# Which matmuls stand at the beginning of a step: reordering the work around a state-space scan

## The chip, the cores and the metric

One core of one Trainium2 chip runs the whole program. The metric is the device time of one execution in microseconds, the median of several runs. Beside it stands one execution taken by the hardware profiler; its page and its trace are what the text quotes.

## The reference, cut to what matters

Four layers with a residual sum around each, on x of 8 x 384 x 32 x 32 in fp32. Each layer first normalizes in 32 groups (`_gn`).

```python
def _mamba(xseq, ...):                      # layer 0; layer 2 adds a layer norm before and an MLP after
    xz = xseq @ in_proj_w.T
    xin, z = jnp.split(xz, 2, axis=-1)      # 768 channels each
    u = silu(conv3(xin))                    # causal, three taps
    dt, Bm, Cm = split(u @ x_proj_w.T)
    dt = softplus(dt @ dt_proj_w.T + dt_proj_b)
    A = -jnp.exp(A_log)                     # 768 x 16
    def step(h, inp):                       # over the 1024 positions
        h = exp(dt_t[..., None] * A) * h + (dt_t * u_t)[..., None] * B_t[:, None, :]
        return h, einsum('bdn,bn->bd', h, C_t)
    y = (ys + u * D) * silu(z)
    return y @ out_proj_w.T

x = x + layer0(_gn(x))                      # _mamba
x = x + layer1(_gn(x))                      # 1x1, 8x8 rfft filter, 3x3 depthwise, gelu gate, 1x1
x = x + layer2(_gn(x))                      # layer norm, _mamba, MLP with gelu
x = x + layer3(_gn(x))                      # 3x3 depthwise
```

## The kernel before, in words

**Chunks and steps.** A layer of the `_mamba` kind is cut into 16 chunks: 8 images of 2 halves of 512 positions. A chunk has 24 steps (NQ), so the two such layers have 768 steps. A step holds 32 channels with their 16 states each, as four tiles of 128 rows by 512 positions. The first half of an image leaves its last states in `carry` for the second.

**One step** has these parts, written in this order by the loop at the end of the function, which is the order on every engine (nothing is rescheduled):

- `times(t+1)`: GpSimd multiplies the loaded dt·u of the next step by B (two products of 2.36 us).
- `scan(t)`: VectorE runs four `tensor_tensor_scan` on the decays dA0 to dA3 (PSUM tiles), multiplies the first two results by C; GpSimd multiplies the other two (L660).
- `jobs.begin`, then `jobs.step(t, 2.0)`: up to about 2 us of TensorE work of other jobs.
- `gather(t-1)`: TensorE sums the states of the step before into y (four matmuls of 32 columns); every fourth step it adds u·D, and VectorE multiplies by the gate z (L676).
- `begin(t+3)`: SyncE loads g, a 1 MB broadcast of the step three ahead, from `dud`. If that step's dt isn't computed yet, `jobs.until` writes whatever job pieces are due first, until it is.
- `jobs.step(t)`: more pieces of other jobs.
- `decay(t+1)`: TensorE spreads dt into dA0 to dA3, ScalarE takes the exponentials in place.

There is one set of dA tiles: the decays of the next step wait for the scans and products of this one.

**Other jobs** are Python generators; a piece runs to the next `yield`. `measure` and `group_stats` take group statistics; `front` is the normalization, in-projection (ps_in, emptied by ScalarE into u, then two tap operations of VectorE), Silu, x-projection (ps_x, dbc), spreading of B and C (ps_bc) and the softplus of dt (ps_dt, three ScalarE operations, then VectorE's dt; GpSimd's du; the write to `dud`); `gates` is z; `finish` is the out-projection and the MLP (ps_up emptied by ScalarE, ps_dn by VectorE); `layer1` and `layer3` are the convolutional layers (ps_t, ps_dw, ps_o). Layer 1 and layer 3 of an image run beside later chunks.

`Jobs` keeps them in the order of their due step (`last`). It meters the TensorE and VectorE work that is written (`work`), and a step has room for so much of either (ROOM). `step` starts a job's next piece where the room is at least what that piece took the last time. The yields are: WAIT (cannot go on), NEXT (go on in the next step), EARLY (go on at the beginning of the next step: Silu and Gelu, with the loading of their ScalarE tables), and None.

**Banks.** Other work has three PSUM banks (`psg`, NBANK = 3). `pipe` passes units through their stages with a bank each, at most `deep` at a time; `live["ps"]` counts the banks that are taken, and `ps_done` counts one free when the instruction that empties it has been written. Only the semaphores, at run time, make a matmul wait for the emptying itself.

Of the kernel before, what the change touches and what calls it, by code (L numbers as in the profile page):

```python
# [48 lines left out]

SHARE = {"l0_": ((2, 2, 2, 2), (2, 2, 2, 2)), "l2_": ((2, 2, 2, 2), (2, 2, 2, 2))}  # L50
# [15 lines left out]
EARLY = "early"  # L66

ROOM = {"l0_": (5.2, 3.0), "turn": (6.4, 3.0), "l2_": (6.4, 3.0)}
# [21 lines left out]
class Jobs:  # L90
# [3 lines left out]

    def __init__(self, work):
        self.work, self.jobs, self.needs = work, [], {}
        self.room = [0.0, 0.0]

    def add(self, kind, gen, first, last):
        self.jobs.append({"kind": kind, "gen": gen, "first": first, "last": last, "had": [], "got": None})  # L100
# [5 lines left out]
    def piece(self, job):  # L106

        before = list(self.work)
        got = next(job["gen"], self)
        if got is WAIT:  # L110
            return False
        took = tuple(x - y for x, y in zip(self.work, before))
        job["had"].append(took)
        self.room = [x - y for x, y in zip(self.room, took)]
        job["got"] = got
        if got is self:
            self.needs[job["kind"]] = job["had"]
            self.jobs.remove(job)
        return True
# [4 lines left out]
    def begin(self, room):  # L124
        self.room = [max(min(x, y / 8), -y) + y for x, y in zip(self.room, room)]
        early = [job for job in self.in_order() if job["got"] is EARLY]
        for job in self.jobs:
            if job["got"] is NEXT:
                job["got"] = None
        if early:  # L130
            self.piece(early[0])

    def step(self, t, most=None):

        most = most and self.work[0] + most
        went = True
        while went and not (most and self.work[0] >= most):
            went = False
            for job in self.in_order():
                need = self.need(job)  # L140
                if job["got"] is None and job["first"] <= t and all(
                    y == 0 or x >= y - 0.1 for x, y in zip(self.room, need)
                ):
                    went = self.piece(job)
                    if went:
                        break

    def until(self, done):

        while not done():  # L150
            if not any(self.piece(job) for job in self.in_order()):
                raise RuntimeError("no job goes on")


@with_exitstack
def tile_conv_preact_d4(ctx: ExitStack, tc: tile.TileContext, a: dict, out: bass.AP):
# [10 lines left out]
    live = {"ps": 0, "dt": 0, "x": 0, "spm": False}  # L167
# [21 lines left out]
    def pipe(units, deep=2):  # L189


        flying = []
        units = deque(units)
        while units or flying:
            went = bool(flying)
            for f in list(flying):
                if f["stages"]:
                    f["stages"].popleft()(f["ps"])
                settle(f)
                if not f["stages"]:  # L200
                    flying.remove(f)
            if units and live["ps"] < NBANK and len(flying) < deep:
                went = True
# [3 lines left out]
                stages[0](ps)  # L207
                f = {"stages": deque(stages[1:]), "ps": ps, "bank": True}
                settle(f)
                if f["stages"]:  # L210
                    flying.append(f)
            if units or flying:
                yield None if went else WAIT

    def settle(f):
        if f["bank"] and (not f["stages"] or f["stages"][0] is None):
            f["bank"] = False
            ps_done()
            if f["stages"]:
                f["stages"].popleft()  # L220
# [59 lines left out]
    def group_stats(block, all_read=lambda: None, between=None):  # L280
# [3 lines left out]
        for h in range(2):  # L284
            for k in range(KC):
                v, then = block(h, k)
                vector.bn_stats(st[:, k, h, :], v)
                then()
# [75 lines left out]
    def depthwise(pool, rows, todo):  # L364
# [13 lines left out]
        for q, (n, t) in enumerate(taps):  # L378
            if t == 0:
                ps = yield from ps_tile("ps_dw")  # L380
            _, window, take = todo[n]
            ready.append(diagonal(q + 3))
            mm(
# [6 lines left out]
            if t % 3 == 2:  # L390
                yield
# [7 lines left out]
    def measure(s):  # L399
# [12 lines left out]
        live["spm"] = True  # L412
# [7 lines left out]
        def all_read():  # L420
            live["spm"] = False
# [3 lines left out]
    def project(s, d, at):  # L425


        def run(ps):
            for k in range(KC):
                mm(  # L430
                    ps,
                    s["w"]["in"][:, k, at + d * P : at + (d + 1) * P],
                    s["xn"][:, k, :],
                    start=k == 0,
                    stop=k == KC - 1,
                )

        return run

    def gates(s, h):  # L440
# [7 lines left out]
        def evict(d):  # L448
# [3 lines left out]
            ("ps_z", [both(project(s, h * NH + d, DI), evict(d))]) for d in range(NH)  # L452
        )
        yield EARLY
# [5 lines left out]
    def layer_norm(xn):  # L460
        ps = yield from ps_tile("ps_ln")
        for k in range(KC):
            mm(ps, ln_mean, xn[:, k, :], start=k == 0, stop=k == KC - 1)
# [4 lines left out]
        while live["spm"]:  # L468
            yield WAIT
        ps = yield from ps_tile("ps_lv")  # L470
        for k in range(KC):
            sq = wk.tile([P, T], F32, tag="spm", name="sq", bufs=2)
            act(sq, xn[:, k, :], AF.Square)
            mm(ps, ln_mean, sq, start=k == 0, stop=k == KC - 1)
        rsqrt(ps, ps, eps_ln)
        yield
# [8 lines left out]
        yield NEXT  # L485

    def front(s):

        c, n = s["c"], s["n"]
        while n > 0 and ("gates", 1) not in chunks[n - 1]:  # L490
# [28 lines left out]
        def taps(d):  # L519
# [9 lines left out]
        yield from pipe(  # L529
            ("ps_in", [both(project(s, d, 0), tap(d), taps(d))]) for d in range(ND)  # L530
        )
# [19 lines left out]
        for d in range(ND):  # L551
            mm(ps[:RX, :], w["x"][:, d, :], u[d], start=d == 0, stop=d == ND - 1)
        dbc = wk.tile([RX, T], F32, tag="dbc", name="dbc")
        act(dbc, ps[:RX, :], AF.Identity, bias=one_row)
        ps_done()
        yield NEXT
# [9 lines left out]
        def step_dt(d):  # L566
# [10 lines left out]
            def plus(ps):  # L577
                v = s["dt"][d] = wk.tile([P, T], F32, tag="dt", name="dt", bufs=NDT)
                vector.scalar_tensor_tensor(v, ps, 0.0, got["m"], ALU.max, ALU.add)

# [11 lines left out]
            return [both(log, plus), None, both(times_u, spill)]  # L592
# [3 lines left out]
        flying = []  # L596
        for d in range(ND):
            while live["dt"] >= NDT or live["spm"]:
                yield WAIT
            live["dt"] += 1  # L600

            flying.append(pipe([("ps_dt", step_dt(d))]))
            flying = [f for f in flying if next(f, f) is not f]
            yield NEXT
        while flying:
            flying = [f for f in flying if next(f, f) is not f]
            yield NEXT
# [29 lines left out]
    def scan(s, i):  # L637

        g = s["g", i]
        own = SHARE[s["pre"]][s["c"]][i % NSUB]  # L640
        for j in range(4):
            q = 4 * i + j
            nc.vector.tensor_tensor_scan(  # L643
                dAs[j] if j < own else g[:, j, :],
# [6 lines left out]
            if j < own:  # L651
                if s["c"] < NCH - 1:
                    nc.vector.tensor_copy(carry[:, q : q + 1], dAs[j][:, T - 1 : T])
                nc.vector.tensor_mul(g[:, j, :], dAs[j], s["bc"][:, 1, :])  # L654
        if s["c"] < NCH - 1:
            nc.vector.tensor_copy(  # L656
                carry[:, 4 * i + own : 4 * i + 4].unsqueeze(2), g[:, own:4, T - 1 : T]
            )
        g = g[:, own:4, :]
        nc.gpsimd.tensor_mul(  # L660
            g, g, s["bc"][:, 1, :].unsqueeze(1).to_broadcast([P, 4 - own, T])
        )

    def gather(s, i):
# [8 lines left out]
        if sub == NSUB - 1:  # L673
            u = s["u"][k // NH][:, k % NH, :]
            mm(y, s["w"]["D"][:, k, :], u, start=False)
            nc.vector.tensor_mul(u, y, s["z", k // NH][:, k % NH, :])  # L676
# [4 lines left out]
    def out_proj(s):  # L681
# [14 lines left out]
        def part(m, h):  # L696
            def run(ps):
                for d in range(h * NH, (h + 1) * NH):
# [474 lines left out]
```

## Time and profile before

| what | value |
|---|---|
| median of 3 runs | 7934.5 us (7925.13 to 7950.72) |
| the profiled execution | 7942.61 us, its span 7940.8 us |
| mean granted TensorE clock | 0.919 of full rate |
| TensorE busy | 7334.3 us, 92% |
| VectorE busy | 5717.7 us, 72% |
| GpSimd busy | 5639.5 us, 71% |
| ScalarE busy | 4052.0 us, 51% |
| DMA queues | 57.2% of 16 engines' span, 1117.98 MB on SyncE's |
| g loads (1 MB each) | 768, 7.1 us from issue to landing |

The span runs from the first instruction to the last; the time of the execution is 1.8 us longer. A matmul's end is modelled, and one that waits behind another is counted busy, so the share of TensorE is no measure of how full it is. An fp32 matmul has two records in the trace. Lines of the program are those of the kernel before; L177 is the helper `mm`, L85 the metered VectorE call, L241 the helper `act`, so the tiles' names tell operations apart.

### The profile page before, as it was taken

The numbers are of one execution on the slowest core, as the hardware profiler recorded it, in microseconds if no ns is written. First come the engines' busy times: TensorE is split into PE (matmuls) and PEld (weight loads), VectorE is DVE, ScalarE is ACT, GpSimd is POOL, SyncE is SP. The second block draws the span as 40 slices with busy tenths as digits, with TensorE's granted clock in tenths as the row PEclk, the third lists the DMA queues.
The fourth block names the chain that finished last, engine by engine and source line by source line (L and its number), as shares of the span: only waits on it lengthen the run. The fifth ranks groups of instructions, "written<-read, shape, count | busy, mean of one in ns | idle before, by whom it ended". The sixth has DMA issues, their size and how long they took to land. (4 is left out here: it accounts for less than half of the span.)

```text
span 7940.8 us, 76871 instructions
## 1 busy us (share of the span) xinstructions
PE 7334.3 (92%) x25954; PEld 3037.2 (38%) x25954; DVE 5717.7 (72%) x7254; ACT 4052.0 (51%) x6980; POOL 5639.5 (71%) x2710
## 2 busy tenths in 40 slices
PE   7989999999998999989999989999899989999898
PEld 2223333333333333333334444444444444344445
DVE  5988788878787878778737647767767676676770
ACT  4445545555555555554544545555555555555553
POOL 5888888877787878777737746767767667676770
PEclk8888888989898999989889989999999999999999
DMA  5665655555564656556526645666656666565662
GB/s 138 148 148 137 144 135 136 134 133 137 133 149 118 146 129 143 122 141 151 122 69 173 159 121 144 154 158 165 157 134 163 166 149 159 138 171 140 168 157 65
DMA packets 289704, 1122.90 MB, mean 141 GB/s; under 512 B 37402, under 2 KB 91754, under 8 KB 191004
## 3 DMA queue, kind: packets, MB, share of 16 engines
q1 hardware_dynamic: 289308, 1117.98, 57.2%
q8 instruction: 205, 3.36, 0.2%
q14 instruction: 191, 1.56, 0.1%
HBM read 1042.34 MB, written 75.50 MB: 141 GB/s over the span
## 5 line engine op out<-in xcount | busy, mean ns | idle before, releaser
L623 POOL TENSOR_TENSOR g<-g,bc 128x1024 f32<-128x1024 f32 x1536 | 3586.5, 2357 | 181.3 <-DMA g<-dud 164.4
L660 POOL TENSOR_TENSOR g<-g,bc 128x1024 f32<-128x1024 f32 x768 | 1805.8, 2351 | 1609.5 <-DVE carry L656 871.8
L241 ACT ACTIVATE dA<-dA,w_A 128x512 f32<-128x512 f32 x3072 | 1858.3, 661 | 1480.3 <-PE dA L177 1467.3
L177 PE MATMUL dA<-dt,selr 32*128 32x512 f32 x6144 | 1521.9, 676 | 67.8 <-DVE g L654 59.2
L643 DVE TENSOR_TENSOR_SCAN dA<-dA,carry,g 128x512 f32<-128x512 f32 x768 | 986.7, 1285 | 750.5 <-issue 375.4
L643 DVE TENSOR_TENSOR_SCAN dA<-dA,g 128x512 f32<-128x512 f32 x768 | 940.8, 1225 | 554.3 <-ACT dA L241 221.6
L654 DVE TENSOR_TENSOR g<-dA,bc 128x512 f32<-128x512 f32 x1536 | 1054.5, 687 | 29.8 <-DVE dA L643 0.5
L177 PE MATMUL y<-g,sely 128*32 128x512 f32 x6144 | 934.2, 640 | 47.6 <-POOL g L660 42.4
L643 DVE TENSOR_TENSOR_SCAN g<-dA,carry,g 128x512 f32<-128x512 f32 x768 | 940.4, 1266 | 0.0
L643 DVE TENSOR_TENSOR_SCAN g<-dA,g 128x512 f32<-128x512 f32 x768 | 893.7, 1206 | 0.0
L177 PEld LDWEIGHTS dA<-dt,selr 32*128 32x128 f32 x6144 | 452.1, 192 | 947.2 <-DVE g L643 473.9
L177 PE MATMUL ps_up<-t,mw 128*128 128x256 f32 x2304 | 605.4, 411 | 144.4 <-ACT h L241 100.5
L177 PE MATMUL ps_dn<-h,mw 128*128 128x256 f32 x2304 | 566.1, 397 | 67.7 <-DMA mw<-in_l_mlp_w 55.9
L177 PE MATMUL ps_z<-xf,w_in 128*128 128x512 f32 x1152 | 590.0, 653 | 27.8 <-DVE dt L85 24.0
L177 PE MATMUL ps_dw<-tp,diag 96*96 96x512 f32 x1152 | 580.7, 645 | 14.3 <-ACT diag L241 14.3
L177 PEld LDWEIGHTS ps_up<-t,mw 128*128 128x128 f32 x2304 | 444.9, 201 | 371.0 <-ACT h L241 186.7
L177 PE MATMUL ps_in<-xf,w_in 128*128 128x512 f32 x1152 | 556.2, 623 | 25.3 <-DVE u L85 22.0
L177 PE MATMUL ps_out<-u,w_out 128*128 128x512 f32 x1152 | 548.7, 623 | 9.1 <-DVE x L85 9.1
L177 PEld LDWEIGHTS ps_dn<-h,mw 128*128 128x128 f32 x2304 | 436.7, 196 | 260.3 <-issue 121.0
L177 PE MATMUL ps_dw<-xp,diag 128*128 128x512 f32 x864 | 405.4, 620 | 41.0 <-ACT diag L241 40.9
L241 ACT ACTIVATE h<-ps_up,vec 128x256 f32<-128x256 f32 x384 | 177.3, 474 | 442.7 <-PE ps_up L177 442.4
L241 ACT ACTIVATE u<-ps_in,w_vec 128x512 f32<-128x512 f32 x192 | 149.4, 778 | 478.1 <-PE ps_in L177 478.1
(98 smaller groups left out, 6514.5 us busy)
## 6 DMA issues: line engine op xcount, KB each, us to landing
g<-dud SPq DMA_DIRECT2D x768, 1024.0 KB, 7.1
mw<-in_l_mlp_w SPq DMA_DIRECT2D x384, 384.0 KB, 7.2
dud<-du SPq DMA_DIRECT2D x768, 64.0 KB, 1.7
xk<-in_x SPq DMA_DIRECT2D x48, 256.0 KB, 4.1
xf<-in_x SPq DMA_DIRECT2D x16, 768.0 KB, 8.5
x<-in_x SPq DMA_DIRECT2D x16, 768.0 KB, 8.4
x_mid<-x SPq DMA_DIRECT2D x16, 768.0 KB, 4.7
xk<-x_mid SPq DMA_DIRECT2D x48, 256.0 KB, 5.4
```

The source lines that it names most:

```text
L177: nc.tensor.matmul(out_, lhsT, rhs, start=start, stop=stop)
L241: nc.scalar.activation(out_, in_, func, **kw)
L623: nc.gpsimd.tensor_mul(g, g, s["bc"][:, 0, :].unsqueeze(1).to_broadcast([P, 2, T]))
L643: nc.vector.tensor_tensor_scan(dAs[j] if j < own else g[:, j, :], dAs[j], g[:, j, :], 0.0 if s["c"] == 0 else carry[:, q : q + 1], ALU.mul ...
L654: nc.vector.tensor_mul(g[:, j, :], dAs[j], s["bc"][:, 1, :])
L660: nc.gpsimd.tensor_mul(g, g, s["bc"][:, 1, :].unsqueeze(1).to_broadcast([P, 4 - own, T]))
```

## The change

No instruction is added or removed on TensorE, VectorE, ScalarE, GpSimd or SyncE, apart from waits on semaphores; the arithmetic stays. What changes is the order.

- **LEAD**: a new yield and a new mark in a unit's list of stages. It stands ahead of the last matmuls of a unit that VectorE empties: ps_in (last third), ps_dt, ps_dn (last third), ps_out of layer 0 (last third), ps_o, the spectra of ps_t, ps_ln, ps_lv, and the last tap of ps_dw. Such a stage runs only in `jobs.step(t, LEADING, lead=True)`, the first 2.7 us of a step, or where work is forced. Then come up to 0.8 us of other pieces (BEFORE), `gather`, and the rest. A step with an EARLY piece has neither.
- `pipe` runs one stage for each call, not one of every unit.
- Pieces are finer: projections in 2 + 1, the out-projection in three parts, a depthwise tap by itself; ps_dn has two units at a time.
- A piece starts where half of what it took before is left as room; ROOM and what is carried over change.
- `until` takes the kind of job that is late and goes on with that alone as far as it can; z's gates are forced at the product with z (new function `gated`) and no longer before the scan; a g load that is three steps ahead is left for the next step when its dt is missing.
- Some NEXT become None: after dbc, after the layer norm's last operation. The out-projection is a job of its own; layer 1 gets a due step first in the list; the softplus's GpSimd product is written straight behind dt, its write to `dud` a step later.

```diff
+LEADING, BEFORE = 2.7, 0.8
+ROOM = {"l0_": (5.8, 2.4), "turn": (6.6, 2.4), "l2_": (6.6, 2.4)}
 ...
     def begin(self, room):
+        self.now += 1
+        self.room = [max(min(x, 0.8), -y / 2) + y for x, y in zip(self.room, room)]
 ...
+    def step(self, t, most=None, lead=False):
+        self.leading = lead
 ...
+                if (
+                    job["at"] <= self.now
+                    and job["got"] is not EARLY
+                    and (job["got"] is LEAD) == lead
+                    and job["first"] <= t
+                    and all(y == 0 or x >= y / 2 for x, y in zip(self.room, self.need(job)))
+                ):
 ...
+    def until(self, done, kind=None):
+        self.leading = True
         while not done():
+            late = [job for job in self.in_order() if job["kind"] == kind]
+            if not any(self.piece(job) for job in late + self.in_order()):
 ...
     def pipe(units, deep=2):
+        def mark(f):
+            stages = f["stages"]
+            f["lead"] = False
+            while stages and stages[0] in (None, NEXT, LEAD):
+                got = stages.popleft()
+                if got is None:
+                    f["bank"] = False
+                    ps_done()
+                elif got is NEXT:
+                    f["at"] = jobs.now + 1
+                else:
+                    f["lead"] = True
+
+        def go(f):
+            f["stages"].popleft()(f["ps"])
+            mark(f)
+            if not f["stages"]:
+                if f["bank"]:
+                    ps_done()
+                flying.remove(f)
+
+        def able(leading):
+            for f in flying:
+                if f["at"] <= jobs.now and (leading or not f["lead"]):
+                    return f
+            if units and live["ps"] < NBANK and len(flying) < deep:
+                return (leading or units[0][1][0] is not LEAD) and units
+            return None
 ...
+        def inward(d):
+            first, last = project(s, d, 0, tap(d))
+            return [first, LEAD, both(last, taps(d))]
+
+        yield from pipe((("ps_in", inward(d)) for d in range(ND)), deep=NBANK - 1)
 ...
-            return [both(log, plus), None, both(times_u, spill)]
+            return [LEAD, both(log, plus, times_u), None, NEXT, spill]
 ...
-        elif s["c"] == NCH - 1:
-            until = 2 * NQ + 3 if s["n"] == B * NCH - 1 else 3 * NQ - 2
-            jobs.add("layer1", layer1(s), 0, t + until)
+        elif s["c"] == NCH - 1:
+            jobs.add("layer1", layer1(s), 0, t + NQ)
 ...
-                return [sum_up(0, 0), sum_up(0, 1), sum_up(1, 0), both(sum_up(1, 1), add)]
+                return [sum_up(0, 0), sum_up(0, 1), sum_up(1, 0), LEAD, both(sum_up(1, 1), add)]
-            yield from pipe([("ps_dn", down(m)) for m in range(KC)], deep=1)
+            yield from pipe([("ps_dn", down(m)) for m in range(KC)])
 ...
-        if i % (NH * NSUB) == NSUB:
-            jobs.until(lambda: ("gates", i // (NH * NSUB)) in s)
         if t + 1 < total:
             times(*steps[t + 1])
         scan(s, i)
         jobs.begin(ROOM["turn" if n == B * NCH else s["pre"]])
-        jobs.step(t, 2.0)
+        early = jobs.early()
+        if not early:
+            jobs.step(t, LEADING, lead=True)
+            jobs.step(t, BEFORE)
         if t > 0:
             p, q = steps[t - 1]
+            h = q // (NH * NSUB)
             gather(p, q)
+            if q % NSUB == NSUB - 1:
+                jobs.until(lambda: ("gates", h) in p, "gates%d" % h)
+            gated(p, q)
 ...
+        while begun < min(t + AHEAD + 1, total):
+            p, q = steps[begun]
+            def ready():
+                return QUADS[q][0] in p.get("dud", {})
+            if begun == t + AHEAD and not ready():
+                break
+            jobs.until(ready, "front%d" % (p["pre"] == "l2_"))
             begin(p, q)
+            begun += 1
         jobs.step(t)
```

## The prediction

> **What bounds the kernel now.** I read the page's head first, then the waits of TensorE, then the timeline of single steps, then the windows with the granted clock.
>
> ```profile
> span 7940.8 us, 76871 instructions
> PE 7334.3 (92%) x25954; PEld 3037.2 (38%) x25954; DVE 5717.7 (72%) x7254; ACT 4052.0 (51%) x6980; POOL 5639.5 (71%) x2710
> L177 PE MATMUL dA<-dt,selr 32*128 32x512 f32 x6144 | 1521.9, 676 | 67.8 <-DVE g L654 59.2
> ```
>
> TensorE looks 92% busy, but that counts a matmul that stands and waits. At full rate the instruction order holds 6010 us of matmul work: 0.43 us per record of 512 columns (6 records of ps_z take 2.84 us below), 1.06 us for a step's four sums of states, the same for its four decays. VectorE has 5718 us. The 768 steps run from the first scan at 92.4 us to about 7742 us: 7650 us, 9.97 each, so neither engine fills a step. Each waits for the other once: TensorE's decays need the tiles dA0 to dA3 back from the scans; the scans need the decays and ScalarE's exponentials.
>
> The only other place where TensorE meets VectorE is a PSUM bank that VectorE has yet to empty. The waits of TensorE show that today it is rare, yet dear:
>
> ```profile
> PE ps_up L177 <- ACT h L241: 100.5, 77, 4.8
> PE ps_z L177 <- DVE dt L85: 24.0, 6, 4.4
> PE ps_in L177 <- DVE u L85: 22.0, 27, 3.9
> PE ps_t L177 <- DVE dt L85: 10.2, 4, 3.3
> ```
>
> The columns are total us, times, longest. One of the six is in the timeline (start, duration, engine, line, operation; in brackets the idle time before and its releaser):
>
> ```profile
> 1254.46 1.29 DVE L643 TENSOR_TENSOR_SCAN dA<-dA,carry,g 128x512 f32<-128x512 f32 x1 [0.93 <-issue]
> ...
> 1255.95 1.06 PE L177 MATMUL y<-g,sely 128*32 128x512 f32 x8
> ...
> 1260.68 0.67 DVE L85 SCALAR_TENSOR_TENSOR dt<-ps_dt,spm 128x512 f32<-128x512 f32 x1
> ...
> 1261.40 4.54 PE L177 MATMUL ps_z<-xf,w_in 128*128 128x512 f32 x6 [4.38 <-DVE dt L85]
> ...
> 1265.87 1.14 PE L177 MATMUL dA<-dt,selr 32*128 32x512 f32 x8
> ...
> 1267.78 1.29 DVE L643 TENSOR_TENSOR_SCAN dA<-dA,carry,g 128x512 f32<-128x512 f32 x1 [5.50 <-issue]
> ...
> 2018.36 2.84 PE L177 MATMUL ps_z<-xf,w_in 128*128 128x512 f32 x6
> ```
>
> ```profile
> 6414.70:6430.20 15.50, 10.85 (x41) 6.25 (x40) 6.32 (x10) 8.13 (x11) 12.24 (x9) 0.78 0.47 120
> ```
>
> The dt operation stands in VectorE's queue behind the step's four scans, so ps_z gets its bank only at 1261.4. TensorE stands 4.38 us; then its six records take 4.54 us where six took 2.84 at 2018.36. The step lasts 13.3 us (1254.46 to 1267.78) with 7.2 us of matmuls. The line below it is a window (us, busy time of PE, PEld, DVE, ACT, POOL, clock 0.78, DMA): a step in which TensorE stands 4.09 us for ScalarE behind a Silu, and again the clock is down.
>
> **What the Trainium skill says.** "TensorE: Matmul & The Clock Gate", Part 2, step 1: matmuls stay in program order, only weight loads are pulled ahead; so a matmul that waits for a bank holds the sums and decays behind it. The trace agrees (1261.40, then 1265.87). The same page, "Architectural detail", has ScalarE and VectorE strictly first in, first out: what is written behind the scans is done behind them (1260.68). The same page, "What's actually happening": after an idle window of some 3.4 us the array drops to half rate for about as long. The trace agrees: 4.54 against 2.84 us. "Perfetto Trace Analysis", "Optimization Strategy", reads a repeated gap as a sign that PSUM ran out of tiles.
>
> **The change, part by part.** Every instruction count stays (12977 matmuls, 6690 activations, 2177 DMAs); the order moves. I went through both instruction orders step by step: matmuls at the durations above and 0.94 of full rate (windows of the 24-step stretches show 0.82 to 0.97); a scan 1.2 to 1.3 us, a product 0.6, other VectorE work columns/830; and each TensorE wait for VectorE, put behind that work. A step costs the largest of TensorE's sum, VectorE's sum plus 0.4, and TensorE's sum with such waits in it.
>
> 1. *Where the work lies.* The forced lumps go: before, single steps hold 104, 58, 28.6, 23.5 (twice) and 33.7 (five times) us of matmuls; after, the largest is 40.1, the next 20.0. But a lump was dense, and the new order makes TensorE steps of 9 to 11 us beside steps of 2 to 5. Without waits the sums over steps are 6787 us before and 6968 after: **+181**. The tail behind the last scan falls from 152.7 to 132.2 us of matmuls: **-22**.
>
> 2. *Banks behind the scans.* A LEAD piece runs at the start of the step, and its emptying by VectorE is written behind the scan of the same step. `pipe` counts the bank free as soon as that is written (ps_done), so the next unit takes it in the same step, and with NBANK = 3 others are held by units that stop before their last part. Example (layer 2, second half of a pair, step 13): ps_in x1, ps_dn x3, ps_in x2, sums, ps_in x2. The second ps_in waits for the taps on the first, behind the scans: about 1.3 + 6.9 + 1.5 = 9.7 us after the decays, where TensorE is after 2.8. All after it, the sums and decays too, waits: 15 us for a step of 8.2. Before, 34 steps hold such a wait, 82 us together; after, 225 steps, 1162 us (89 in layer 0 and the turn, 453 us; 136 in layer 2, 709 us): u taps 528, dt 191, residual adds x 186, gate 101, tpix 79, acc 59, xf 16. As steps: 74 us before, 1091 after: **+1017**. From the decays' end to the scan the timeline shows 0.85 us, not 1.3: 0.45 x 191 more steps = **-86**.
>
> 3. *Half rate after the gap.* 170 steps stand 3.4 us or longer, 8 before. At 1.7 us each (4.54 - 2.84): 162 x 1.7 = 275; bound 0 (a low window may hold no matmul) to 400. I take **+220**.
>
> 4. *What improves.* The steps' sum with waits is 6861 of 7650 us, so 789 us are lost otherwise: 83 in the 13 steps where ps_up stands behind Silu (6.4 each; 4 such steps after: -58), about 150 with dt, xf and x consumers written late in front of a scan (to be hidden), and the rest spread at 1 us per step. In a step that already stands for a bank that loss falls into the gap: 191 x 1.0 = -191. **-370** in all, bound -100 to -650.
>
> 5. *Queues.* SyncE's dud writes move a step behind du, g loads may be issued a step later: two steps are still 18 us, against 7.1 us to land. GpSimd's du comes straight behind dt: it was 71% busy. Both at nothing, at most +50.
>
> Sum: 7942.6 (the profiled execution, 8 above the median of 7934.5) + 181 - 22 + 1017 - 86 + 220 - 370 = 8883; less 8 for the median, **8875 us**, 12% slower.
>
> **Rivals.** *Faster (7%).* The waits are there in order but not in time: VectorE is at the consumer when TensorE needs the bank. Then 7942 + 181 - 22 - 370 = 7730. It decides where the mean stand falls under 1.1 us in 191 steps (+211). For it: ps_in's 27 waits above have a mean of 0.8. Against: those units stand a step apart; 34 steps of the kernel before that hold such a wait by the same count last 12.8 us in the mean, 11.7 reckoned (five of them 10.3 for 10.6).
> *Milder (16%).* Half the waits' price, since TensorE's earlier work in a step is slower than reckoned, and the late consumers give all back: 7942 + 181 + 508 - 22 - 300 = 8310.
> *Worse (12%).* The clock stays low also between gaps, at 0.85 instead of 0.92 over 6010 us: +540 instead of 220, near 9200.
> *The order is not what the words say (2%).* The order of the two programs rules out that nothing moved.
>
> **How the numbers follow.** My own case has 63%, 8500 to 9200; the range 8400 to 9230 leaves out the faster case, half of the milder one and part of the worse. About 0.3% (24 us) is what can be told from no change. Faster 0.07, same 0.02, slower 0.91.
>
> **What would show it.** Right: waits "ps_in, ps_dt, ps_dn, ps_z, ps_up <- DVE" of 5 to 7 us in TensorE's list, over 900 us together with the weight loads' list; granted clock under 0.9; VectorE's share falling to about 64%; no step over 60 us. Wrong in step 2: these waits stay under 200 us. Wrong in step 4: steps without such a wait last 1 us or more over their sums, as now.

## The result and the profile after

The kernel after takes **9636.5 us** (median of 4 runs, 9631.3 to 9642.2) against 7942.6 us for the kernel before (4 runs): a ratio of 1.2135, interval 1.2108 to 1.2162. It is 21% slower; the prediction had 12%, and its range ended at 9230 us. The direction and the main mechanism were right, the sum was 761 us short.

The page of the kernel after: its head, and the row of the granted clock, one digit for a fortieth of the span, in tenths.

```profile
span 9640.5 us, 77147 instructions
PE 7972.1 (83%) x25954; PEld 3160.4 (33%) x25954; DVE 5719.3 (59%) x7254; ACT 4068.6 (42%) x6980; POOL 5627.8 (58%) x2710
...
PEclk8888888888888888878888888888888888888889
```

The same row in the page of the kernel before:

```profile
PEclk8888888989898999989889989999999999999999
```

Every engine's work is what it was (VectorE 5719 us, ScalarE 4069), and every share has fallen. The clock, 0.9 in most of the second half before, is at 0.8 nearly throughout: 0.849 in the mean, against 0.919. The waits of TensorE in the kernel after (us in total, times, longest; here `mm` is L193, `act` L283, the metered VectorE call L85 as before, the scans L716, GpSimd's product for the sums L731):

```profile
PE ps_in L193 <- DVE u L85: 320.2, 47, 7.7
PE ps_dt L193 <- DVE dt L85: 194.9, 52, 8.5
PE ps_up L193 <- ACT h L283: 115.0, 147, 5.0
PE y L193 <- POOL g L731: 92.7, 67, 7.3
...
PE ps_dw L193 <- DVE gate L85: 59.1, 9, 11.1
PE ps_dw L193 <- DVE u L85: 49.6, 7, 7.6
...
PE ps_in L193 <- DVE x L85: 42.3, 19, 4.9
```

ps_in's wait for VectorE's taps, 22.0 us before, is 320.2, and its mean is 6.8 us, not 0.8. ps_dt's wait for dt was 5.4. The wait of ps_up behind ScalarE, which the prediction hoped to see shrink, has not (100.5 before). One of the new waits in the timeline, a step of layer 2 (start, duration, engine, line, operation; in brackets the idle time before and its releaser):

```profile
8381.70 1.12 PE L193 MATMUL ps_in<-xf,w_in 128*128 128x512 f32 x2
...
8382.53 1.23 DVE L716 TENSOR_TENSOR_SCAN dA<-dA,g 128x512 f32<-128x512 f32 x1 [9.30 <-issue]
...
8388.84 1.53 DVE L85 SCALAR_TENSOR_TENSOR u<-ps_in,w_vec,u 128x511 f32<-128x511 f32 x2
...
8390.52 3.75 PE L193 MATMUL ps_in<-xf,w_in 128*128 128x512 f32 x4 [7.69 <-DVE u L85]
...
8394.20 1.06 PE L193 MATMUL y<-g,sely 128*32 128x512 f32 x8
...
8396.68 1.14 PE L193 MATMUL dA<-dt,selr 32*128 32x512 f32 x8
...
8398.59 1.23 DVE L716 TENSOR_TENSOR_SCAN dA<-dA,g 128x512 f32<-128x512 f32 x1 [8.22 <-ACT dA L283]
```

The LEAD part of one ps_in (two records) is done at 8382.8. VectorE's taps on it start at 8388.84, behind the four scans. The next ps_in was given that bank and waits 7.69 us; its four records then take 3.75 us, where two took 1.12. The sums and the decays stand behind it. The step lasts 16.1 us (8382.53 to 8398.59) and holds some 6 us of matmuls (six records of ps_in at 0.43 us, sums and decays at 1.06 each, six records of ps_dn at 0.22).

**Where TensorE's time went.** For the stretch from the first scan to the last, the time from each matmul's start to the next was divided: the time at full rate; what the half clock added; and the rest, put down, where it was over 0.25 us, to the engine whose semaphore update came last. In us:

| | before | after | change | e1 | e14 | e15 | e10 | e12 |
|---|---|---|---|---|---|---|---|---|
| first scan to last scan | 7650 | 9364 | +1714 | 8375 | 7977 | 7759 | 7464 | 7456 |
| matmuls at full rate, breaks under 0.25 us | 5106 | 5151 | +45 | 5093 | 5106 | 5108 | 5104 | 5056 |
| half clock | 399 | 786 | +387 | 600 | 428 | 377 | 381 | 334 |
| VectorE, banks | 133 | 1059 | +926 | 176 | 304 | 107 | 122 | 115 |
| VectorE's scans, ScalarE's exponentials | 300 | 339 | +39 | 383 | 306 | 309 | 284 | 210 |
| ScalarE, other | 382 | 515 | +133 | 495 | 383 | 375 | 389 | 385 |
| GpSimd | 72 | 140 | +68 | 237 | 149 | 152 | 45 | 150 |
| DMA | 108 | 15 | -93 | 41 | 8 | 20 | 3 | 41 |
| the rest: what sums and decays take beyond their price here, breaks with no releaser | 1146 | 1355 | +209 | 1349 | 1292 | 1308 | 1135 | 1166 |

The columns e1 to e12 belong to experiments below. The last row is largely work and not idle time. A step's four sums (or decays) are recorded as matmuls that start 0.01 us apart and share 0.43 us; the division priced each at a quarter of that, and what was over fell into this row, its half clock too. Reckoned again, with four such records as one matmul of 0.43 us and the half clock applied to breaks under 0.25 us as well, the same traces give 504 us of half clock before and 1006 after (+502), 105 and 1019 for the banks (+914), and +298 for all else. The half-clock row is thus a lower figure.

### The profile page after: what moved, and what is told of

Same layout as the page of the kernel before. It is cut to its first block, busy times and chain, and to the rows that moved or that the text cites. A ratio compares the mean times of both kernels' runs of the same rounds, so it can differ in the third digit from the quotient of the medians.

```text
span 9640.5 us, 77147 instructions
## 1 busy us (share of the span) xinstructions
PE 7972.1 (83%) x25954; PEld 3160.4 (33%) x25954; DVE 5719.3 (59%) x7254; ACT 4068.6 (42%) x6980; POOL 5627.8 (58%) x2710
## 5 line engine op out<-in xcount | busy, mean ns | idle before, releaser
L731 POOL TENSOR_TENSOR g<-g,bc 128x1024 f32<-128x1024 f32 x768 | 1803.4, 2348 | 3076.1 <-DVE g L716 1651.8
L283 ACT ACTIVATE dA<-dA,w_A 128x512 f32<-128x512 f32 x3072 | 1860.9, 660 | 2475.3 <-PE dA L193 2467.0
L716 DVE TENSOR_TENSOR_SCAN dA<-dA,carry,g 128x512 f32<-128x512 f32 x768 | 987.5, 1286 | 1583.1 <-issue 719.9
L716 DVE TENSOR_TENSOR_SCAN dA<-dA,g 128x512 f32<-128x512 f32 x768 | 940.6, 1225 | 1342.0 <-ACT dA L283 599.0
L193 PE MATMUL dA<-dt,selr 32*128 32x512 f32 x6144 | 1557.3, 702 | 78.1 <-DVE g L727 71.8
L193 PE MATMUL y<-g,sely 128*32 128x512 f32 x6144 | 1094.5, 707 | 115.3 <-POOL g L731 92.7
L193 PE MATMUL ps_in<-xf,w_in 128*128 128x512 f32 x1152 | 728.6, 765 | 414.1 <-DVE u L85 320.2
L716 DVE TENSOR_TENSOR_SCAN g<-dA,carry,g 128x512 f32<-128x512 f32 x768 | 940.4, 1266 | 0.0
L716 DVE TENSOR_TENSOR_SCAN g<-dA,g 128x512 f32<-128x512 f32 x768 | 893.7, 1206 | 0.0
L193 PE MATMUL ps_up<-t,mw 128*128 128x256 f32 x2304 | 634.4, 421 | 184.8 <-ACT h L283 115.0
L193 PEld LDWEIGHTS dA<-dt,selr 32*128 32x128 f32 x6144 | 449.3, 198 | 1002.7 <-DVE g L716 326.8
L193 PE MATMUL ps_dw<-tp,diag 96*96 96x512 f32 x1152 | 611.0, 663 | 121.9 <-DVE gate L85 59.1
L193 PE MATMUL ps_dn<-h,mw 128*128 128x256 f32 x2304 | 600.7, 414 | 85.1 <-DVE x L85 34.1
L193 PE MATMUL ps_z<-xf,w_in 128*128 128x512 f32 x1152 | 589.0, 648 | 98.3 <-ACT z L283 45.3
L193 PEld LDWEIGHTS ps_up<-t,mw 128*128 128x128 f32 x2304 | 456.1, 207 | 413.0 <-ACT h L283 195.1
L193 PE MATMUL ps_out<-u,w_out 128*128 128x512 f32 x1152 | 571.0, 638 | 20.9 <-DVE x L85 17.4
L193 PEld LDWEIGHTS ps_dn<-h,mw 128*128 128x128 f32 x2304 | 466.9, 207 | 302.6 <-issue 165.2
L283 ACT ACTIVATE h<-ps_up,vec 128x256 f32<-128x256 f32 x384 | 181.7, 474 | 856.1 <-PE ps_up L193 856.1
L193 PE MATMUL ps_dw<-xp,diag 128*128 128x512 f32 x864 | 452.3, 660 | 86.8 <-ACT diag L283 53.8
L193 PEld LDWEIGHTS ps_in<-xf,w_in 128*128 128x128 f32 x1152 | 247.5, 233 | 819.4 <-issue 670.4
```

Source lines behind the costliest of these rows:

```text
L193: nc.tensor.matmul(out_, lhsT, rhs, start=start, stop=stop)
L283: nc.scalar.activation(out_, in_, func, **kw)
L716: nc.vector.tensor_tensor_scan(dAs[j] if j < 2 else g[:, j, :], dAs[j], g[:, j, :], 0.0 if s["c"] == 0 else carry[:, q : q + 1], ALU.mult, ...
L731: nc.gpsimd.tensor_mul(g, g, s["bc"][:, 1, :].unsqueeze(1).to_broadcast([P, 2, T]))
```

## The experiments

In e1 to e3 Theory 1 is the prediction's own: banks taken again behind the scans, and the half clock after the gap. Its rival was that chains inside a job grew slower where the change dropped a NEXT.

**e1_hold: the banks alone.** The kernel after, but a bank that a LEAD piece has filled is counted free only when the next step begins.

```diff
     def ps_done():
-        live["ps"] -= 1
+        if jobs.hold:            # a LEAD piece is being written
+            live["held"] += 1
+        else:
+            live["ps"] -= 1
 ...                              # behind jobs.begin:
+        live["ps"] -= live["held"]
+        live["held"] = 0
```

> The kernel after, with one edit in its planner: a bank that a LEAD piece empties through VectorE is counted free only when the next step begins, so no unit takes it in the same step. In the instruction order the steps with a TensorE wait for VectorE work behind the scans fall from 225 to 68, their standing from 1162 to 142 us; the sum over steps with these waits falls from 8059 to 7198 us (7058 without them: the work is more lumped), the tail behind the last scan grows by some 57 us of matmuls. Theory 1 (banks taken again behind the scans, with the half clock after the gap, make the loss): 8400 to 8750 us. Theory 2 (the loss comes from chains that are now written without a step between their parts, dbc to ps_bc and layer norm to ps_in, and from smaller pieces; banks are cheap): 9300 us or more, since none of that is touched.

Measured: 8725.3 us, 1.099 of before (1.0958 to 1.1022). 911 us of the 1694 are gone, and TensorE's time for VectorE's banks falls from 1059 to 176. Theory 1 holds; the rest is not explained by banks.

**e2_nolead: LEAD alone undone.** Every LEAD counts as None, and the first part of a step is `jobs.step(t, 2.0)` as before; finer pieces, the rule of room, forcing by kind and the early du stay.

```diff
-            jobs.step(t, LEADING, lead=True)
-            jobs.step(t, BEFORE)
+            jobs.step(t, 2.0)
```

> The kernel after with LEAD undone: units that VectorE empties may run anywhere in a step, and the beginning of a step again takes up to 2.0 us of whatever is due. The finer pieces, the missing NEXTs, the forcing of late work alone and layer 1's due step stay. In the order 97 steps hold a wait for VectorE work behind the scans (306 us of standing), no step has more than 12 us of matmuls; sum over steps with waits 7164 us. Theory 1: 8250 to 8650 us, so most of the 1700 us goes with LEAD alone. Theory 2: above 9200 us.

Measured: 8236.8 us, 1.0375 (1.0344 to 1.0405). LEAD is worth 1400 of the 1694 us, a little more than Theory 1 expected.

**e3_nexts: the rival alone.** The kernel after with a NEXT again behind dbc, behind the layer norm's last operation, and between its squares and their sums.

> The kernel after with three NEXTs put back: behind dbc, behind the layer norm's last operation, and between its squares and their sums. Bank waits stay: 212 steps, 1070 us; the sum over steps with them falls from 8059 to 7947 us. Theory 1: 9350 to 9600 us. Theory 2: 9000 us or less, most of what the shortened chains cost being won back.

Measured: 9491.8 us, 1.1955 (1.1921 to 1.199): 145 us less than the kernel after. The rival is real, and small.

**e4_clockgap and e9_clockshare: the clock alone.** Bursts of fp32 matmuls 128x512 with pauses in which TensorE waits for VectorE; neither does any of the reference's work, and each was executed once. First nine matmuls to a burst and a longer pause in each row.

> A small kernel by itself, with none of the reference's work: bursts of nine fp32 matmuls 128x512 into one PSUM tile, each burst waiting for VectorE to empty it; between copy and last read VectorE has 0, 2, 3, 4, 5, 6, 8 or 12 products of 0.6 us, sixteen bursts each (tiles ga to gi). Half rate after a gap, as used in step 3 of the prediction (one window of 3.4 us costs 1.7 us): bursts of about 7.7 us while the gap is under 3.4 us, 9.4 us or more above. If a gap costs more than one window: bursts of 11 us and above, up to 15. If the clock doesn't depend on the gap: 7.7 us throughout.

Windows of e4: us, length, busy time of PE, PEld, DVE and POOL, granted clock, DMA. The pauses are 1.5, 2.7, 3.4, 4.9, 5.6, 7.1 and 10.0 us.

```profile
3.60:156.90 153.30, 130.73 (x288) 54.47 (x288) 20.81 (x31) 0.00 (x0) 1.00 0.00 0
158.40:335.40 177.00, 136.34 (x288) 56.37 (x288) 38.70 (x60) 0.00 (x0) 0.95 0.00 0
338.10:534.50 196.40, 144.84 (x288) 59.26 (x288) 49.08 (x76) 0.00 (x0) 0.91 0.00 0
757.40:992.20 234.80, 161.54 (x288) 65.92 (x288) 69.82 (x105) 0.00 (x0) 0.84 0.00 0
997.10:1246.70 249.60, 165.40 (x288) 67.64 (x288) 80.22 (x120) 0.00 (x0) 0.82 0.00 0
1252.30:1517.30 265.00, 159.03 (x288) 65.69 (x288) 100.99 (x150) 0.00 (x0) 0.80 0.00 0
1524.40:1841.00 316.60, 167.03 (x288) 68.13 (x288) 142.56 (x210) 0.00 (x0) 0.75 0.00 0
```

A burst takes 8.0 us after pauses of 1.5 us (all but the first), 10.1 after 4.9 us (161.54/16), 10.3 after 5.6 us (165.40/16): a pause of 5 to 6 us costs 2.1 to 2.3 us. And the clock falls already with pauses of 2.7 us, which none of the three cases expected.

> A measurement of the clock alone; it does none of the reference's work. Bursts of fp32 matmuls 128x512 (0.86 us each) with a pause that two or four VectorE operations make, 40 times each: ha 1 matmul, hb 2, hc 3, hd 5, pause about 1.5 us; he 1, hf 3, hg 6, pause about 2.7 us. No pause reaches 3.4 us. Theory 1 (the share of TensorE's work in a window of 3.41 us decides, not the length of one pause; in the trace of the kernel after, the clock was halved behind 97 to 100% of the windows with under 0.2 of work and behind 7% of those with 0.7 to 0.8): ha (0.36 busy at full rate) and he (0.24) run at half clock most of the time, hb (0.53) partly, hc, hd, hf and hg (0.49 to 0.74) hardly. Theory 2 (only a pause of some 3.4 us halves the clock, as the prediction counted it): all stay at full clock.

Windows of e9: pauses of 1.5 us with bursts of 1, 2, 3 and 5 matmuls, then pauses of 2.7 us with 1, 3 and 6.

```profile
3.60:145.20 141.60, 82.92 (x80) 20.03 (x80) 53.90 (x79) 0.00 (x0) 1.00 0.00 0
146.80:286.60 139.80, 81.10 (x160) 27.55 (x160) 53.72 (x78) 0.00 (x0) 1.00 0.00 0
...
704.40:892.00 187.60, 82.05 (x80) 19.82 (x80) 100.57 (x157) 0.00 (x0) 0.51 0.00 0
894.70:1177.80 283.10, 177.57 (x240) 60.70 (x240) 100.55 (x156) 0.00 (x0) 0.74 0.00 0
1180.50:1553.60 373.10, 267.56 (x480) 105.45 (x480) 100.55 (x156) 0.00 (x0) 0.86 0.00 0
```

The 1.00 of the first row is no measurement: this trace has no record of the clock before 151.0 us, and the view counts such time as full clock. How long a single matmul takes tells more. Three of them, one from the first row's stretch (ha) and two from the stretch that begins at 704.40 (he), on either side of its change to half clock:

```profile
10.76 2.08 PE L34 MATMUL ha<-x,w 128*128 128x512 f32 x2 [1.50 <-DVE s L38]
...
704.41 1.13 PE L34 MATMUL he<-x,w 128*128 128x512 f32 x2 [1.50 <-DVE s L38]
708.24 2.07 PE L34 MATMUL he<-x,w 128*128 128x512 f32 x2 [2.71 <-DVE s L38]
```

The first matmul of he still has full clock (the record of half clock begins at 707.4) and takes 1.13 us; the next, at half clock, 2.07. All forty of the first row take 2.04 to 2.08: they ran at half clock, and their pauses of 1.5 us never let it rise. Bursts of two, three and five with the same pauses had full clock from 151.0 us on. So Theory 2 fails. Theory 1 has ha, he, hc and hd right; hb, which it put partly at half clock, had full clock once it had risen, and hf (some 0.5 of work) was at half clock for half of its time.

What share of work decides can be read from these two traces, though no run was made to test it. The clock's records lie on a grid of 3.41 us. At full clock, each window of the grid in which TensorE was busy for 0.41 or less of the time was followed by one at half clock (164 of 164), and each with 0.42 or more by one at full clock (495 of 495). At half clock, where the same work takes twice as long, it stayed there below 0.78 (115 of 115) and rose above 0.83 (149 of 149). In the kernel after, too, all 194 windows at full clock with less than 0.40 were followed by half clock; many with more were as well (156 of 1762), but there a matmul that waits can count as busy.

**e5_fill: the half clock inside the kernel after.** In 122 of the 171 places where TensorE is reckoned to stand 3 us or more, matmuls of a zero weight were added into y (which they don't change), so that TensorE works for 514 us of the time it would stand.

```diff
     def mm(out_, lhsT, rhs, start=True, stop=True):
 ...
+        for _ in range(FILL.get(live["mm"], 0)):   # place in the order -> how many
+            nc.tensor.matmul(y, zero, eye broadcast to 512 columns, start=False, stop=False)
+        live["mm"] += 1
```

> The kernel after, with 598 extra matmuls of a zero weight (0.86 us each, 514 us in all) added into y in 122 of the 171 places where TensorE is reckoned to stand 3 us or more for a bank that is emptied behind the scans (in the other places y is not open). They change no value; they shorten the standing to 1.7 to 2.6 us, too short for much of the half rate. Theory 1 (the half clock after the gap is the term that was priced too low; a gap of 5 to 7 us costs 2.0 to 2.4 us in the clock measurement): 122 x 2.2 = 270 us less, 9300 to 9450 us, granted clock 0.87 or more. Theory 2 (what the prediction missed lies in other waits, for ScalarE, GpSimd, and breaks between units; the clock is only a symptom): within 60 us of the kernel after, 9580 to 9700. Rival to both: the stand was reckoned too long and the extra work comes on top, 9700 or more.

Measured: 9489.9 us, 1.1953 (1.1923 to 1.1983), clock 0.886: 147 us less than the kernel after, between the two theories. The extra work took the place of the standing (banks 1059 to 597 us, matmuls at full rate +512), and the half clock fell from 786 to 619. Pauses of 2 us or more fell from 289 to 194: 167/95 = 1.8 us of half clock each (2.0 by the second reckoning). So in these places the half clock is a cause and no symptom, at about the price of the prediction. Doing 514 us of useless work in these places gained 147 us.

**e14_pref and e15_pref_hold: place or ban.** LEAD does two things: such pieces come first in a step, and they may come nowhere else. e14 keeps the first and drops the second.

```diff
-                    and (job["got"] is LEAD) == lead
+                    and (lead is None or (job["got"] is LEAD) == lead)
 ...
-        jobs.step(t)
+        jobs.step(t, lead=None)          # LEAD pieces too
         if t + 1 < total:
             decay(*steps[t + 1])
```

> The kernel after, with LEAD pieces taken first at the beginning of a step, as there, but allowed in the rest of the step as well. All else stays, the banks too. The sum over steps with waits is 7164 us (after: 8059), 90 steps wait for a bank (225). Theory 1 (the ban in the rest of the step is what costs: it heaps these pieces on the beginnings, where their banks are taken again at once, and leaves the rest of the steps empty): 8180 to 8320, as without LEAD (8237). Theory 2 (the place at the beginning, in front of the sums, costs by itself): 8600 or more.

> The kernel of e14, and a bank that VectorE empties counted free only in the next step, as in e6. Sum over steps with waits 7030 (e6: 6974). Theory 1 (as for e14): 7030 + 707 other losses as in e6 + 270 before and behind the loop = 8007, 7950 to 8070, against 8725 with the ban. Theory 2 (the place costs by itself): 8300 or more.

Measured: e14 8248.6 us, 1.0388 (1.0364 to 1.0413); e15 8025.9 us, 1.0102 (1.0073 to 1.0131). Both agree with Theory 1. As a two by two:

| | bank free at once | VectorE's bank free in the next step |
|---|---|---|
| LEAD pieces only at the beginning | 9636.5 (after) | 8725.3 (e1; LEAD's banks) |
| LEAD pieces first at the beginning, also later | 8248.6 (e14) | 8025.9 (e15) |

The ban costs 1388 us with the banks free at once and some 700 without. The place at the beginning costs little: without any LEAD the same two columns are 8236.8 (e2) and 7950.0 (e6), 12 and 76 us less. In e14 (page and waits of TensorE) the clock row lies between those of before and after (0.896 in the mean), and ps_in's wait for the taps, 320.2 us in the kernel after, is 7.3:

```profile
PEclk7878888898889888898999999899998999999999
```

```profile
PE ps_dt L193 <- DVE dt L85: 85.6, 31, 4.6
...
PE ps_in L193 <- DVE u L85: 7.3, 5, 3.7
```

**e11_hold_front2: are the sums uncovered?** The kernel of e1 with `LEADING, BEFORE = 2.7, 2.0`.

> The kernel of e1 (LEAD, its banks free only in the next step; 8725 us), with one number changed: up to 2.0 us of other pieces instead of 0.8 ahead of the sums. The sums over steps hardly change (7215 with waits, against 7198). Theory 1 (LEAD loses because the sums stand uncovered in front of GpSimd's product and leave windows with little work): TensorE's wait for GpSimd (237 us) falls below 180 and the clock rises, 8450 to 8620. Theory 2 (the loss lies in what LEAD forbids and then forces: work gathered in lumps and steps without any): within 60 us of e1, 8660 to 8790.

Measured: 8670.5 us, 1.093 (1.0903 to 1.0957), clock 0.886 (e1: 0.883). The wait for GpSimd went from 237 to 196 us only. It is 55 us less than e1, within Theory 2: the number ahead of the sums is not what e1 mainly loses.

**e8, e10 and e13: the early du.** The change writes GpSimd's du straight behind dt, and the write to `dud` a step later. The prediction priced this at nothing. In e8 it is undone in the kernel of e7 (below), in e13 in the kernel after; in e10 it is done in the kernel before, and nothing else is.

```diff
-            return [both(log, plus), None, both(times_u, spill)]      # before
+            return [both(log, plus, times_u), None, spill]            # e10
```

> The kernel of e7, with GpSimd's product for dud a step later, as before, instead of straight behind dt. Nothing else moves. Theory 1 (GpSimd's place of du costs nothing): within 30 us of e7. Theory 2 (GpSimd's product for the sums stands behind du, which waits for dt behind the scans; TensorE's wait for it is 169 us without LEAD against 72 before): 50 to 100 us less than e7.

> The kernel before, with one edit: GpSimd's du stands straight behind VectorE's dt, its write to dud a step later (as in the kernel after), instead of both a step later. No other instruction moves on any engine. Theory 1 (SyncE stands in its queue for du and holds up the weights and g loads behind it; the late du cost 156 us in e8): TensorE's waits for the DMA of mw fall from 108 to under 40 us and the kernel takes 50 to 150 us less, 7790 to 7890. Theory 2 (the price in e8 belongs to that order alone; du is hidden in the kernel before, as the prediction's step on the queues had it): within 25 us of before.

> The kernel after, with GpSimd's du a step later, next to its write to dud, as in the kernel before. The sums over steps do not change (8058 us with waits, against 8059). Theory 1 (the early du takes SyncE's stand away in every one of these orders: 176 us in the kernel before, 156 in e7): 9750 to 9830, so that the other parts of the change cost more than the difference of the two kernels shows. Theory 2 (steps of 12 us leave the queue time enough, du is hidden): 9600 to 9680.

Measured: e8 8041.5 us against e7's 7885.1 (+156): both theories fail, the late du costs. **e10 7755.0 us, 0.9773 of before (0.9749 to 0.9796)**: one line, 2.3% faster than the kernel before, a little more than Theory 1 expected. e13 9701.5 us (1.2222, 1.2191 to 1.2253): 65 us more than the kernel after, between its two theories. Waits in the kernel before, then in e10 (SPq is SyncE's queue; L590 is the write to dud, L623 is `times`):

```profile
SPq L590 <- POOL du L583: 1726.6, 183, 47.7
...
POOL g L623 <- DMA g<-dud: 164.4, 116, 14.1
```

```profile
SPq L590 <- POOL du L583: 996.2, 161, 47.7
...
POOL g L623 <- DMA g<-dud: 18.1, 7, 13.8
```

In the trace SyncE issues in the order written. While its write of dud waits for a du that GpSimd has not come to (47.7 us at the longest, with nothing issued in that time), the g loads and the MLP's weights behind it wait too. With du a step ahead of the write that standing falls by 730 us, GpSimd no longer waits for g (164.4 to 18.1), and TensorE's waits for mw are gone (108 us to 3 in the table).

**e6, e7 and e12: without LEAD, and better than before.** e6 is e2 with VectorE's banks free only in the next step. e7 adds the old rule of room and coarse pieces. e12 changes one number of e7, VectorE's room in a step.

```diff
-                    and all(y == 0 or x >= y / 2 for x, y in zip(self.room, self.need(job)))
+                    and all(y == 0 or x >= y - 0.1 for x, y in zip(self.room, self.need(job)))
 ...
-ROOM = {"l0_": (5.8, 2.4), "turn": (6.6, 2.4), "l2_": (6.6, 2.4)}
+ROOM = {"l0_": (5.2, 3.0), "turn": (6.4, 3.0), "l2_": (6.4, 3.0)}   # e7; 2.6 in l0_ and l2_ in e12
```

> The kernel without LEAD of the second experiment (8237 us), and every bank that VectorE empties is counted free only when the next step begins. Same work. Theory 1 (what the kernel without LEAD still loses against before is the same wait: 97 steps with 306 us of standing, against 34 with 82): 23 steps with 37 us remain, the sum over steps with waits goes from 7164 to 6974, so about 190 us less, 8000 to 8100. Theory 2 (the loss comes from finer pieces and from sums that wait for GpSimd): 8180 or more.

> The kernel of e6, and the old rule for when a piece has room (all of what it took before, the old ROOM and carry-over), and the old coarse pieces of projections and convolutions. The sum over steps with waits is 6756 us (before: 6861, after: 8059), the tail 177 us (before: 153). With the other losses as in the kernel without LEAD (1072 us over its sum): 6756 + 1072 + 47 = 7875. Theory 1 (the sum of the steps decides, and the other losses stay where they are): 7800 to 7930, faster than before. Theory 2 (evenly dealt work raises the other losses, since fewer steps have work to spare): 7990 or more.

> The kernel of e7 (7885 us) with VectorE's room a step 2.6 us instead of 3.0. Sum over steps with waits 6753 (e7: 6756), tail 145 us of matmuls instead of 177. If the sum and the tail decide: 7850, faster than before by 1.2%. If evenly dealt VectorE work brings waits of its own: 7900 or more.

Measured: e6 7950.0 us, 1.0007 (1.0 to 1.0014), 287 us under e2 where 190 were expected: the bank waits fell by 229 us in the trace (291 to 62), the half clock by 71 (443 to 372). e7 7885.1 us, 0.9928 (0.9906 to 0.995), as Theory 1 had it (7875). **e12 7740.2 us, 0.9748 (0.9722 to 0.9774)**, 110 us better than expected. In e12's trace the half clock is 42, ScalarE's waits 60 and GpSimd's 24 us lower than in e7; why one number does that was not tested. e10 and e12 beat both kernels, by about the same.

## Why the prediction was right or wrong

**Step 1, where the work lies (+181, tail -22): not contradicted, not measured alone.** The tail behind the last scan is 182 us long after 199: -17. The +181 of steps that VectorE fills would show as waits for scans and exponentials; these rose by 39 only, and the late consumers of step 4 lie in the same row.

**Step 2, banks behind the scans (+1017 - 86 = +931): right.** The table has +926. That they differ by 5 us is chance, for one is how much longer steps get and the other how long TensorE stands. What was predicted for a step of this kind, 15 us with the sums and decays held up, is the 16.1 us shown above. e1 removes the waits with one edit.

**Step 3, half rate (+220): the mechanism and nearly the price right, the count too low; +387 measured, +502 by the second reckoning.** The price of 1.7 us came from one example; e5 gives 1.8 to 2.0, e4 2.1 at 5 us. But the step counted only the 162 added stands of 3.4 us or longer. There are 187 more pauses of 2 us or more than before (289 against 102), and 387/187 = 2.1 us. The prediction took the threshold from the Trainium skill, "TensorE: Matmul & The Clock Gate", "What's actually happening", an idle window of some 3.4 us; in e4 and e9 a pause of 2.7 us was enough (0.51 to 0.95), for a window with 0.41 of work or less already cost the clock; the measurement decides.

**Step 4, what improves (-370): this is the step that failed.** Its three parts add up to -399, of which it took -370; none of them came. The prediction itself said what would show it wrong: steps without a bank wait that last 1 us or more over their sums. They do, 542 steps by 1.50 us in the mean, where before all steps lay 1.03 over. The losses beyond the sum over steps with waits, from first scan to last scan, were

| kernel | after | e1 | e3 | e13 | before | e2 | e6 | e7 | e14 | e15 | e12 | e10 |
|---|---|---|---|---|---|---|---|---|---|---|---|---|
| the ban | yes | yes | yes | yes | no | no | no | no | no | no | no | no |
| loop | 9364 | 8375 | 9187 | 9424 | 7650 | 7959 | 7681 | 7559 | 7977 | 7759 | 7456 | 7464 |
| sum with waits | 8059 | 7198 | 7947 | 8058 | 6861 | 7164 | 6974 | 6756 | 7164 | 7030 | 6753 | 6861 |
| loop - sum | 1305 | 1177 | 1240 | 1366 | 789 | 795 | 707 | 803 | 813 | 729 | 703 | 603 |

Wherever LEAD pieces may stand only at the beginning, 1177 to 1366 us are lost beyond the sum (1122 in e11, whose loop is 8337); in the eight kernels without that ban 603 to 813 (970 in e8, with its late du and a loop of 7726). So the sums with their waits missed above all the ban, and after it the place of du (e10 has the sum of before). The prediction had 419 + 220 - 86 = 553 here, where 1305 were lost. Its three terms: ps_up behind ScalarE still waits (131 us before, 140 after, in TensorE's accounts); a gain from the late consumers is not seen in the scans' row; and the losses did not fall into the gaps, for the 225 steps with a bank wait lost 1305 - 542 x 1.50 = 492 us, 2.2 each, half clock included. Taken together, steps 1 and 4 were to give 181 - 370 = -189; the rows of the table other than banks and half clock give +401. That is 590 of the 761 us, and step 3 is most of the rest (167); by the second reckoning it is 487 (+298) and 282. Either way step 4 is the largest part.

Why the ban costs is shown as far as e14 and e15 go: it is the ban. How is read from the traces, not tested further. Pieces that VectorE empties heap up in the first part of some steps, and other steps are left nearly empty: of 347 steps of layer 2, 12 held under 7 us of TensorE work before, 51 after, 87 in e1, 34 in e15. The loss lies in the full steps. Among the steps without a bank wait, those with 9 us of matmuls or more last 14.3 us in the kernel after (121 steps) and 15.5 in e1 (166), 3.3 and 3.5 us over the larger of TensorE's work at 0.94 of full rate and VectorE's plus 0.4 us; in e15 (164) it is 1.3. The steps under 7 us lie within 0.2 us of that measure in all three. From e1 to e15 half clock falls by 223 us, ScalarE's waits by 120, GpSimd's by 85, scans and exponentials by 74.

**Step 5, queues (nothing to +50): wrong, in sign.** The early du gained 65 us in the kernel after (e13), 156 in e7, 176 in the kernel before (e10). The waits of before had the sign: GpSimd waited 164.4 us for g, and SyncE 1726.6 for du. The prediction looked at the 18 us between write and load, and not at what else stands in SyncE's queue. It made the kernel after look better than its other parts are.

**The rivals.** The clock of 0.85, by which "worse" was to be told, was measured (0.849). Its price for the half clock, +540 in place of +220, is near the second reckoning's +502. Its mechanism, a low clock between the gaps too, holds in part at most: in the 564 steps where the trace shows no bank wait the half clock adds 0.99 us each, against 0.63 before. That is some 200 us of the 502; the rest is in the steps with a bank wait, and filling some of those waits raised the clock to 0.886 (e5). VectorE's share came to 59% (64 predicted). "No step over 60 us" missed narrowly: one has 62.0, where before had 128.9.

## What to carry to other kernels

A buffer is free when the work that empties it is done, not when it is written: where that work stands in a queue behind long instructions, give the buffer out again a step later (here -287 us without LEAD, -911 with it). A preference for a place in the order was cheap here (12 and 76 us), a ban from all other places was not (1388 and some 700); try the preference first. Before a product that a DMA waits for is called hidden, look at everything behind that DMA in its issuing queue.

## What the runs showed of the hardware that was not expected

- In e4 and e9 the clock followed the share of work in windows of 3.41 us, and not the length of one pause: at full clock 0.41 or less halved it, at half clock it took more than some 0.8 to raise it again. Pauses of 2.7 us therefore gave a mean clock of 0.51, 0.74, 0.86 and 0.95 with one, three, six and nine matmuls between them.
- Time that has no clock record is counted as full clock: the single matmuls of e9's first row show 1.00 and ran at half clock, 2.07 us where 1.13 are taken at full clock.
- Useless matmuls in TensorE's gaps made a kernel faster (e5, 147 us), since more of the work behind the gaps ran at full rate (half clock 786 to 619 us).
